# Experts' scatters and gathers interleaved, gate products and a batch's values moved in the slot plan

## The chip, the core and the metric

The kernel runs on one core of a Trainium2 chip. The metric is the device time of one execution in microseconds (us); lower is better. The engines are called as in the profile: PE (TensorE matmul, with its weight load PEld), DVE (VectorE), ACT (ScalarE), POOL (GpSimd) and SP (SyncE, which here issues most of the DMAs).

## What is computed

The input x has 4 batches of 1024 rows with 128 channels. Cut to what matters, the reference is:

```
xn  = layernorm(x)
x   = x + attention(xn) + ffn(xn)

attention: 16 heads of 8 channels; scores q.k + two relative-position terms (63 buckets,
           clipped at +-31), softmax, values + a relative-position value term, projection
ffn:       scores = softmax(xf @ gate_w.T); the 6 best of 64 experts for each row
           xb[e, pos] = xf[tok]                      # at most 64 rows for each expert
           h  = silu(xb @ w1.T) * (xb @ w3.T)        # 64 experts, inner width 88
           y[tok] += (h @ w2.T) * weight             # scatter-add
           z  = silu(xf @ ws1.T) * (xf @ ws3.T) @ ws2.T     # shared expert, width 176
```

All of it is float32.

## The kernel before

Attention is cut into 16 units: unit u is batch u // 4 with four heads, u % 4. `period(u)` issues one unit's work in 32 slots, numbered k = 0 to 31. In every slot PE computes far scores of unit u (p2, exponentiated on ACT at L616) woven with far scores of unit u + 1 (p1, whose row maxima DVE takes at L570). Around these two, a hand-written plan of slots places everything else: values of the unit (`values`, an even slot each), scores near the diagonal (`near_keys`, step "a", and others), masks, row maxima and loads. Every engine works through its own queue in the order in which the program issues to it. So the place of a call in a slot sets the order on PE, DVE, ACT, POOL and in the DMA queues.

Two PSUM pools are passed round: `ps2` with two pairs of banks (p2, the shared expert's pz, a batch's pv, the near products pkb and others) and `ps1` with three single banks (p1, the experts' pxg, ph and py, the shared expert's pzo and others). A buffer is handed out again once its reader has finished.

POOL's queue, in the units with experts, holds these in turn: the masking of rows at slots 4 and 5 (`residues`, L476, products km and qm, which PE's pkb matmuls of slot 9 take), a multiplication of the finished unit (o, L700) at slot 9, the additions of maxima to near scores (nt, L643) at slots 12 and 31, masks again at slots 18 and 19, and the indirect DMAs of the experts.

The 64 experts are done in 16 batches of four, two batches for each unit from 5 on, by `moe(u, k)`, which advances a generator `experts`. An even batch flips its gathered rows (pxg) at slot 27, computes the gates (ph, tanh on ACT, two products on DVE) at slot 31, and in the next unit's slot 2 the outputs (py, scaled on DVE into yw, L324). An odd batch does so at slots 17, 19 and 25. A batch's step at slot 2 or 25 is followed by `load_experts` for the batch after next: three weight loads on SP, then four gathers on POOL (L297). The four scatter-adds into y_rows (L327, on POOL) are issued at slot 6 for an even batch and at slot 26 for an odd one. As they add to the same array, each waits until the one before has landed. The first two batches' loads and eight gathers are issued in unit 5 at slot 20.

The shared expert (`shared`) takes, at slots 3, 5, 7 and 13, a product pz with its gates (tanh on ACT, two products on DVE into zs, L283 to L285), and then pzo. At the head of a batch (u % 4 == 0) the values of the whole batch are computed: `batch_values`, in slots 1, 3, 5, 7, 9 for the far form and 4, 6, 8, 10 for the near one, behind the experts' step of the slot.

Of the kernel before, what the change touches and what calls it, by code (L numbers as in the profile page):

```python
# [11 lines left out]
AF = mybir.ActivationFunctionType  # L12
# [12 lines left out]
E, TOPK, CAP, FI, SI = 64, 6, 64, 88, 176  # L25
# [15 lines left out]
def attention_moe_kernel(ctx: ExitStack, tc: tile.TileContext, ins: dict, out: bass.AP):  # L41
    nc = tc.nc
    pe, act, dve, pool = nc.tensor, nc.scalar, nc.vector, nc.gpsimd
# [3 lines left out]
    def mm(o, lhsT, rhs, start, stop=True):  # L47
        pe.matmul(o, lhsT, rhs, start=start, stop=stop, skip_group_check=True)  # L48
# [39 lines left out]
    xs_d = nc.dram_tensor("xs_rows", (T + 1, C + E), F32).ap()  # L88
# [80 lines left out]
    gather_i = cp.tile([CAP, E], I32, name="gather_i")  # L169
# [110 lines left out]

    def silu_mul(o, h1, h3):

        act.activation(o, h1, AF.Tanh, scale=0.5)  # L283
        dve.scalar_tensor_tensor(o, o, 1.0, h1, ALU.add, ALU.mult)
        dve.scalar_tensor_tensor(o, o, 0.5, h3, ALU.mult, ALU.mult)  # L285

    def load_experts(mp, q):
        es = slice(4 * q, 4 * q + 4)
        w1 = mp.tile([C, 4, FI], F32, tag="w1", name=f"w1_{q}")
        w3 = mp.tile([C, 4, FI], F32, tag="w3", name=f"w3_{q}")  # L290
        w2 = mp.tile([FI, 4, C], F32, tag="w2", name=f"w2_{q}")
        nc.sync.dma_start(w1, ins["w1"][:, es, :])
        nc.sync.dma_start(w3, ins["w3"][:, es, :])
        nc.sync.dma_start(w2, ins["w2"][:, es, :])
        xg = mp.tile([CAP, 4, C + E], F32, tag="xg", name=f"xg{q}")
        for e in range(4):
            pool.indirect_dma_start(  # L297
                out=xg[:, e, :], out_offset=None, in_=xs_d[:, :],
                in_offset=bass.IndirectOffsetOnAxis(ap=gather_i[:, 4 * q + e : 4 * q + e + 1], axis=0),
            )  # L300
        return w1, w3, w2, xg

    def experts(mp, q, w1, w3, w2, xg):

        px = bank(f"pxg{q}")
        for e in range(4):
            flip(px[:, CAP * e : CAP * e + CAP], xg[:, e, 0:C], e == 0)
        xgT = mp.tile([C, 4 * CAP], F32, tag="xgT", name=f"xgT{q}", bufs=1)
        dve.tensor_copy(xgT, px[:, 0 : 4 * CAP])
        yield  # L310
        ph = bank(f"ph{q}").rearrange("p (k x) -> p k x", k=2)
        for k, w in ((0, w1), (1, w3)):
            for e in range(4):
                mm(ph[0:FI, k, CAP * e : CAP * e + CAP], w[:, e, :], xgT[:, CAP * e : CAP * e + CAP], e == 0 and k == 0)
        hs = mp.tile([FI, 4 * CAP], F32, tag="hs", name=f"hs{q}", bufs=1)
        silu_mul(hs, ph[0:FI, 0, :], ph[0:FI, 1, :])
        yield
        py = bank(f"py{q}")
        yw = mp.tile([CAP, 4, C], F32, tag="yw", name=f"yw{q}", bufs=1)
        for e in range(4):  # L320
            mm(py[0:CAP, C * e : C * e + C], hs[:, CAP * e : CAP * e + CAP], w2[:, e, :], e == 0)
        x = C + 4 * q
        for e in range(4):
            dve.tensor_scalar_mul(yw[:, e, :], py[0:CAP, C * e : C * e + C], xg[:, e, x + e : x + e + 1])  # L324
        yield
        for e in range(4):
            pool.indirect_dma_start(  # L327
                out=y_d[:, :], out_offset=bass.IndirectOffsetOnAxis(ap=scatter_i[:, 4 * q + e : 4 * q + e + 1], axis=0),
                in_=yw[:, e, :], in_offset=None, compute_op=ALU.add,
            )  # L330
        yield

    def shared(k):
        b, c = divmod(k, 2)
        xc = xnT[:, b, PAD + 512 * c : PAD + 512 * c + 512]
        for f in range(2):
            zs = wk.tile([FI, 512], F32, tag="zs", name=f"zs{k}_{f}", bufs=1)
            pz = psum(f"pz{k}_{f}")
            for j, w in enumerate((later["ws1"], later["ws3"])):
                mm(pz[0:FI, j, :], w[:, FI * f : FI * f + FI], xc, True)  # L340
            silu_mul(zs, pz[0:FI, 0, :], pz[0:FI, 1, :])
            yield
            po = bank(f"pzo{k}_{f}")
            for t in range(4):
                mm(po[:, C * t : C * t + C], zs[:, C * t : C * t + C], later["ws2"][:, f, :], t == 0)
            xv = xacc[:, 8 * b + 4 * c : 8 * b + 4 * c + 4, :].rearrange("p n c -> p (n c)")
            dve.tensor_tensor(xv, xv, po, ALU.add)
            yield
# [39 lines left out]
    def batch_values(b, ws):  # L388

        flat = lambda t: t.rearrange("p h r -> p (h r)")  # L390
        ones = one9.unsqueeze(1).to_broadcast([P, 4, 36])
        pv = psum(f"pv{b}_{ws[0]}")
        place = lambda i: (pv[:, i // 3, 144 * (i % 3) : 144 * (i % 3) + 144])
        for i, (far, t) in enumerate(ws):
            k0 = PAD + 128 * t if far else 64 * t
            mm(place(i), xnT[:, b, k0 : k0 + 128], later["w_v"], i % 3 == 0)
        for i, (far, t) in enumerate(ws):
            if far:
                dve.tensor_tensor(vf[:, :, t].rearrange("p a h r -> p a (h r)"), place(i).unsqueeze(1).to_broadcast([P, 2, 144]),  # L399
                                  rv_ul.rearrange("p a g r -> p a (g r)"), ALU.add)  # L400
            else:
                dve.tensor_tensor(flat(vn[:, t]).rearrange("p (g r) -> p g r", r=36), place(i).rearrange("p (g r) -> p g r", r=36),
                                  ones, ALU.add)

    def first_values(u):
        for a in range(2):
            dve.tensor_copy(v0s[u % 2][:, a, :, 0:9], vf[:, a, 0, 4 * (u % 4) : 4 * (u % 4) + 4, :])
# [309 lines left out]
    pools = []  # L717
    loaded = {}
# [35 lines left out]
    quads = {}  # L754

    def moe(u, k):

        n = u - 5
        if not 0 <= n <= E // 8:
            return  # L760
        q = {2: -2, 6: -2, 17: -1, 19: -1, 25: -1, 26: -1, 27: 0, 31: 0}.get(k, -E) + 2 * n
        if 0 <= q < E // 4:
            if k in (17, 27):
                quads[q] = experts(pools[0], q, *loaded.pop(q))
            next(quads[q], None)
            if k in (2, 25) and q + 2 < E // 4:
                loaded[q + 2] = load_experts(pools[0], q + 2)
        if k in (3, 5, 7, 13) and n < E // 8:
            if k == 3:
                quads["shared"] = shared(n)  # L770
            next(quads["shared"])
# [43 lines left out]
    def period(u):  # L815
# [10 lines left out]
        for k in range(SLOTS):  # L826
# [16 lines left out]
                last.append(finish_last(u, U, 0))  # L843
            if k in sides:
                next(other, None)
            if k in take_at.get(u, ()):
                next(taking[0], None)
            moe(u, k)
# [11 lines left out]
            if U and k % 2 == 0 and k > 0:  # L860
                values(u, k // 2 - 1)
                if k in (14, 22):
                    tables, products = near_values(u, U, k // 22, wts[u])
                    for emit in tables:
                        emit()
                if k in (16, 24):
                    for emit in products:
                        emit()
            for emit in x:
                emit()  # L870
            r()
# [14 lines left out]
            if U:  # L886
                if k == 1:
                    max_ready(u, U, 1)
                    if V:
                        query_rows(u + 1, V, 1)  # L890
                        replicas(u + 1, V, 0)
                if u % 4 == 0:
                    if k in far_at:
                        batch_values(u // 4, [(True, t) for t in far_at[k]])
                    if k in near_at:
                        batch_values(u // 4, [(False, t) for t in near_at[k]])
                    if k == 1:
                        first_values(u)
                if k == 2:
                    wts[u] = value_table(u)  # L900
                    max_sent(u, U, 1, max_rows(u, U, 1))
                if k == 12:
                    near_shift(u, U, 1)
                    if u == 0:
                        add_bias(0)
                if k in (4, 6, 18, 20):
                    near_exp(u, U, k // 18, k in (6, 20))
# [8 lines left out]
            if u == 5 and k == 20:  # L916
                route_ctx.close()
                pools.append(ctx.enter_context(tc.tile_pool(name="moe", bufs=2)))
                loaded.update({q: load_experts(pools[0], q) for q in range(2)})
            if k == 12 and u + 2 < UNITS:  # L920
                tabs[u + 2] = score_tables(u + 2)
            if k == 30 and u + 2 < UNITS:
# [102 lines left out]
```

## Time and profile before

| | |
|---|---|
| median of 3 runs | 1734.68 us (1733.72 to 1736.65) |
| profiled execution | 1794.26 us |
| its span, first to last instruction | 1792.5 us |
| mean granted TensorE clock in it | 0.961 |
| PE busy | 1654.7 us, 92% of the span |
| DVE, ACT, POOL busy | 57%, 42%, 34% |
| scatters (L327) on POOL | 64, 91.1 us busy, 1424 ns each |
| gathers (L297) on POOL | 64, 59.1 us busy, 923 ns each |
| km (L476) on POOL | 32, 80.2 us busy, 2508 ns each |

The profiled execution is 59.6 us longer than the median of the timed runs. Rows of groups give line, engine, operation, output and input, count, then the busy time and the mean of one in ns, and behind the second bar the idle time of the engine just ahead of them with what ended most of it.

### The profile page before, as it was taken

The page shows a single profiled execution, that of the slowest core. Times are in us where ns is not written, and L with a number is a line of the kernel's source. Part 1 is how long each engine was busy: PE and PEld are TensorE (multiplying, and loading weights), DVE is VectorE, ACT ScalarE, POOL GpSimd, SP SyncE. Part 2 cuts the span into 40 slices and gives each one's busy share as a digit, 9 for nine tenths or more (in the row PEclk, how much of TensorE's full clock was granted, in tenths as well). Part 3 has the DMA queues.
Part 4 walks back from the last instruction along what each step waited for, and adds up shares of the span by engine and source line. Part 5 has one row for each costly group of instructions (what it writes and reads, how often), then busy time and mean ns, then how long its engine had stood idle before and what let it go on. Part 6 is the DMA issues. An engine that isn't in the chain of part 4 may idle for free. (4 is left out here: it accounts for less than half of the span.)

```text
span 1792.5 us, 61397 instructions
## 1 busy us (share of the span) xinstructions
PE 1654.7 (92%) x28106; PEld 1005.9 (56%) x28106; DVE 1030.6 (57%) x1836; ACT 754.3 (42%) x846; POOL 603.0 (34%) x336
## 2 busy tenths in 40 slices
PE   7879989899999997999998999999999899997996
PEld 3645555465656554566565665656656566564652
DVE  5666555666666575554656556555555654554522
ACT  0144434544443452444434345444444433454463
POOL 1042141321457553142333423335252332422330
PEclk8899989999999997999999999999999999998998
DMA  5231331322222132231323223232232322313221
GB/s 143 66 91 44 91 102 42 98 69 69 62 72 72 39 98 60 80 91 50 103 79 84 62 53 103 77 87 74 81 86 64 96 56 71 80 46 102 86 79 31
DMA packets 89002, 136.20 MB, mean 76 GB/s; under 512 B 19156, under 2 KB 57965, under 8 KB 88745
## 3 DMA queue, kind: packets, MB, share of 16 engines
q1 hardware_dynamic: 80137, 126.35, 24.6%
q0 software_dynamic: 7168, 5.25, 2.4%
q8 instruction: 220, 3.60, 0.8%
q10 hardware_dynamic: 1440, 0.70, 0.2%
q14 instruction: 37, 0.30, 0.1%
HBM read 117.68 MB, written 14.55 MB: 74 GB/s over the span
## 5 line engine op out<-in xcount | busy, mean ns | idle before, releaser
L570 DVE TENSOR_REDUCE mx<-p 128x1 f32<-128x480 f32 x992 | 604.2, 650 | 487.7 <-PE p L48 436.5
L616 ACT ACTIVATE et<-p 128x1024 f32<-128x1024 f32 x496 | 507.8, 1025 | 699.4 <-PE p L48 661.3
L48 PE MATMUL p<-qu,kf 32*128 32x512 f32 (+4 forms) x1536 | 332.4, 514 | 37.4 <-DMA qu<-m_rows 7.4
L48 PE MATMUL p<-kf,ql 32*128 32x480 f32 (+8 forms) x1536 | 348.0, 502 | 18.9 <-DVE mx L570 14.8
L48 PE MATMUL p<-ql,kf 32*128 32x512 f32 (+4 forms) x1536 | 312.0, 490 | 13.0 <-DVE xacc L706 5.9
L48 PE MATMUL p<-kf,qu 32*128 32x480 f32 (+8 forms) x1536 | 320.8, 481 | 1.5 <-DVE mx L570 1.5
L643 POOL TENSOR_TENSOR nt<-nt,mb 128x1024 f32<-128x1024 f32 x64 | 154.5, 2425 | 356.6 <-DMA mb<-m_rows 271.5
L48 PE MATMUL acc<-et,vf 128*9 128x512 f32 (+4 forms) x2688 | 245.9, 464 | 2.9 <-DVE vf L399 2.2
L48 PEld LDWEIGHTS p<-qu,kf 32*128 32x128 f32 x1536 | 120.4, 188 | 159.4 <-ACT et L616 40.4
L48 PEld LDWEIGHTS p<-ql,kf 32*128 32x128 f32 x1536 | 132.0, 191 | 80.4 <-issue 27.9
L48 PEld LDWEIGHTS p<-kf,qu 32*128 32x128 f32 x1536 | 142.8, 192 | 23.8 <-issue 11.4
L48 PEld LDWEIGHTS p<-kf,ql 32*128 32x128 f32 x1536 | 133.0, 189 | 39.6 <-DVE mx L570 31.7
L476 POOL TENSOR_TENSOR km<-kr,mask_k 128x1088 f32<-128x1088 f32 x32 | 80.2, 2508 | 190.5 <-DMA kr<-k_rows 177.1
L327 POOL DMA_INDIRECT y_rows<-yw,scatter_i x64 | 91.1, 1424 | 154.8 <-DMA y_rows<-yw,scatter_i 118.1
L502 ACT COPY kb<-pkb 128x1024 f32<-128x1024 f32 x64 | 64.8, 1012 | 162.7 <-PE pkb L48 158.3
L48 PE MATMUL pn<-qm,t 64*128 64x64 f32 x2048 | 130.0, 278 | 0.0
L48 PEld LDWEIGHTS acc<-et,vf 128*9 128x9 f32 x2688 | 51.4, 90 | 139.5 <-issue 127.9
L48 PEld LDWEIGHTS pn<-qm,t 64*128 64x128 f32 x2048 | 121.1, 190 | 10.9 <-issue 10.9
L297 POOL DMA_INDIRECT xg<-xs_rows,gather_i x64 | 59.1, 923 | 198.6 <-issue 145.5
L476 POOL TENSOR_TENSOR qm<-qm,mask_q 128x1024 f32<-128x1024 f32 x32 | 75.5, 2359 | 74.4 <-DMA qm<-q_rows 44.3
L48 PE MATMUL pkb<-kr,qm 64*64 64x64 f32 x4096 | 83.3, 223 | 15.3 <-issue 12.2
L48 PEld LDWEIGHTS pkb<-km,t 64*64 64x64 f32 x4096 | 67.8, 136 | 44.8 <-issue 35.1
(242 smaller groups left out, 1910.3 us busy)
## 6 DMA issues: line engine op xcount, KB each, us to landing
mb<-m_rows SPq DMA_DIRECT2D x64, 512.0 KB
kr<-k_rows SPq DMA_DIRECT2D x64, 272.0 KB
qm<-q_rows SPq DMA_DIRECT2D x64, 256.0 KB
wt<-in_rv_ext SPq DMA_DIRECT2D x16, 1024.0 KB
w<-in_w SPq DMA_DIRECT2D x48, 176.0 KB
rb<-r_rows SPq DMA_DIRECT2D x15, 512.0 KB
t<-in_rk_ext SPq DMA_DIRECT2D x64, 46.0 KB
t<-in_rq_ext SPq DMA_DIRECT2D x64, 46.0 KB
```

The costliest lines, as they stand in the source:

```text
L48: pe.matmul(o, lhsT, rhs, start=start, stop=stop, skip_group_check=True)
L297: pool.indirect_dma_start(out=xg[:, e, :], out_offset=None, in_=xs_d[:, :], in_offset=bass.IndirectOffsetOnAxis(ap=gather_i[:, 4 * q + e : ...
L327: pool.indirect_dma_start(out=y_d[:, :], out_offset=bass.IndirectOffsetOnAxis(ap=scatter_i[:, 4 * q + e : 4 * q + e + 1], axis=0), in_=yw[ ...
L476: pool.tensor_tensor(by8(o), by8(t), mask.unsqueeze(1).to_broadcast([P, t.shape[1] // 8, 8]), ALU.mult)
L502: act.copy(U.kb[p][:, :, :, 64 * gh : 64 * gh + 64], pkb.rearrange("p e (n w) -> p e n w", w=64))
L570: dve.reduce_max(U.mx[:, half, h, n : n + 1], p1[e][:, 0:w], axis=AX.X)
L616: act.activation(et, wide, AF.Exp)
L643: pool.tensor_tensor(U.nt[p, c], U.nt[p, c], mb, ALU.add)
```

## The change

Three things move. First, a batch's step at slot 2 or 25 now issues the loads of the batch after next, and then its four scatters, each followed by one gather for the batch after next; slots 6 and 26 no longer hold scatters. Second, the tanh of the gates is separated from the two DVE products, which are issued one slot later: for the experts at slots 20 and 0 (in place of 19 and 31), for the shared expert at slots 4 and 8 (in place of 3 and 7). Third, `batch_values` and `first_values` stand ahead of the experts' step in their slot. The gathers of the first two batches are issued by the same new function.

```diff
     def silu_mul(o, h1, h3):
 
-        act.activation(o, h1, AF.Tanh, scale=0.5)
         dve.scalar_tensor_tensor(o, o, 1.0, h1, ALU.add, ALU.mult)
         dve.scalar_tensor_tensor(o, o, 0.5, h3, ALU.mult, ALU.mult)
...
         xg = mp.tile([CAP, 4, C + E], F32, tag="xg", name=f"xg{q}")
-        for e in range(4):
-            pool.indirect_dma_start(
-                out=xg[:, e, :], out_offset=None, in_=xs_d[:, :],
-                in_offset=bass.IndirectOffsetOnAxis(ap=gather_i[:, 4 * q + e : 4 * q + e + 1], axis=0),
-            )
         return w1, w3, w2, xg
+
+    def gather(q, e, xg):
+        pool.indirect_dma_start(
+            out=xg[:, e, :], out_offset=None, in_=xs_d[:, :],
+            in_offset=bass.IndirectOffsetOnAxis(ap=gather_i[:, 4 * q + e : 4 * q + e + 1], axis=0),
+        )
...
         hs = mp.tile([FI, 4 * CAP], F32, tag="hs", name=f"hs{q}", bufs=1)
+        act.activation(hs, ph[0:FI, 0, :], AF.Tanh, scale=0.5)
+        yield
         silu_mul(hs, ph[0:FI, 0, :], ph[0:FI, 1, :])
         yield
...
-        yield
+        if q + 2 < E // 4:
+            loaded[q + 2] = load_experts(mp, q + 2)
         for e in range(4):
             pool.indirect_dma_start(
                 out=y_d[:, :], out_offset=bass.IndirectOffsetOnAxis(ap=scatter_i[:, 4 * q + e : 4 * q + e + 1], axis=0),
                 in_=yw[:, e, :], in_offset=None, compute_op=ALU.add,
             )
+            if q + 2 < E // 4:
+                gather(q + 2, e, loaded[q + 2][3])
         yield
...
+            act.activation(zs, pz[0:FI, 0, :], AF.Tanh, scale=0.5)
+            yield
             silu_mul(zs, pz[0:FI, 0, :], pz[0:FI, 1, :])
             yield
...
-        q = {2: -2, 6: -2, 17: -1, 19: -1, 25: -1, 26: -1, 27: 0, 31: 0}.get(k, -E) + 2 * n
+        q = {0: -2, 2: -2, 17: -1, 19: -1, 20: -1, 25: -1, 27: 0, 31: 0}.get(k, -E) + 2 * n
         if 0 <= q < E // 4:
             if k in (17, 27):
                 quads[q] = experts(pools[0], q, *loaded.pop(q))
-            next(quads[q], None)
-            if k in (2, 25) and q + 2 < E // 4:
-                loaded[q + 2] = load_experts(pools[0], q + 2)
-        if k in (3, 5, 7, 13) and n < E // 8:
+            next(quads[q])
+        if k in (3, 4, 5, 7, 8, 13) and n < E // 8:
...
+            if U and u % 4 == 0:
+                if k in far_at:
+                    batch_values(u // 4, [(True, t) for t in far_at[k]])
+                if k == 1:
+                    first_values(u)
             if k in take_at.get(u, ()):
                 next(taking[0], None)
             moe(u, k)
...
+            if U and u % 4 == 0 and k in near_at:
+                batch_values(u // 4, [(False, t) for t in near_at[k]])
             for emit in x:
                 emit()
             r()
...
-                if u % 4 == 0:
-                    if k in far_at:
-                        batch_values(u // 4, [(True, t) for t in far_at[k]])
-                    if k in near_at:
-                        batch_values(u // 4, [(False, t) for t in near_at[k]])
-                    if k == 1:
-                        first_values(u)
...
-                loaded.update({q: load_experts(pools[0], q) for q in range(2)})
+                for q in range(2):
+                    loaded[q] = load_experts(pools[0], q)
+                    for e in range(4):
+                        gather(q, e, loaded[q][3])
```

## Prediction

> **What bounds the kernel now.** I read the page from the top: engines, clock, groups, then the waits, the tiles that the change moves, and last the timelines of POOL and PE in one unit.
>
> ```profile
> span 1792.5 us, 61397 instructions
> PE 1654.7 (92%) x28106; PEld 1005.9 (56%) x28106; DVE 1030.6 (57%) x1836; ACT 754.3 (42%) x846; POOL 603.0 (34%) x336
> L327 POOL DMA_INDIRECT y_rows<-yw,scatter_i x64 | 91.1, 1424 | 154.8 <-DMA y_rows<-yw,scatter_i 118.1
> L476 POOL TENSOR_TENSOR km<-kr,mask_k 128x1088 f32<-128x1088 f32 x32 | 80.2, 2508 | 190.5 <-DMA kr<-k_rows 177.1
> L297 POOL DMA_INDIRECT xg<-xs_rows,gather_i x64 | 59.1, 923 | 198.6 <-issue 145.5
> ```
>
> PE sets the time (92%); POOL is two thirds idle. The 118.1 us in which scatters wait for the landing of the scatter before them are POOL's idle time, so removing them is worth nothing by itself. Two things can count: what else stands in POOL's queue, and what PE waits for. The rows of the mask product km say who waits for it now ("us, times"):
>
> ```profile
> who waited for it (us, times):
>   PEld pkb L48: 3.8, 3
>   PE pkb L48: 3.1, 2
> ```
>
> So PE nearly never waits for km and its partner qm. How near it is, the POOL timeline of unit 9 shows (start, duration, idle before):
>
> ```profile
> 1092.71 0.95 POOL L297 DMA_INDIRECT xg<-xs_rows,gather_i  x1 [3.19 <-DVE yw L324]
> ...
> 1096.42 0.91 POOL L297 DMA_INDIRECT xg<-xs_rows,gather_i  x1 [0.30 <-issue]
> 1103.01 2.48 POOL L476 TENSOR_TENSOR km<-kr,mask_k 128x1088 f32<-128x1088 f32 x1 [5.68 <-DMA kr<-k_rows]
> 1105.45 2.36 POOL L476 TENSOR_TENSOR qm<-qm,mask_q 128x1024 f32<-128x1024 f32 x1
> 1107.97 1.46 POOL L327 DMA_INDIRECT y_rows<-yw,scatter_i  x1 [0.17 <-issue]
> 1116.27 1.45 POOL L327 DMA_INDIRECT y_rows<-yw,scatter_i  x1 [6.84 <-DMA y_rows<-yw,scatter_i]
> 1119.54 1.40 POOL L327 DMA_INDIRECT y_rows<-yw,scatter_i  x1 [1.82 <-DMA y_rows<-yw,scatter_i]
> ```
>
> Today: four gathers, km, qm, and only then the scatters. PE's timeline has the product of kr and qm at 1110.62, 2.8 us after qm ends. The same distance is 1.9, 3.6, 9.9, 2.8, 2.1, 3.2, 11.4 and 0.1 us in units 6 to 13. The third thing to see is PE beside the gathers, in unit 5 (eight of them in a row) and unit 9:
>
> ```profile
> 709.53 0.48 PE L48 MATMUL pkb<-kr,qm 64*64 64x64 f32 x3 [0.97 <-issue]
> 713.08 0.48 PE L48 MATMUL pkb<-kr,qm 64*64 64x64 f32 x4 [1.14 <-issue]
> 705.80:719.50 13.70, 9.38 (x155) 5.51 (x158) 1.22 (x2) 2.04 (x2) 4.59 (x6) 0.50 0.19 52
> ```
>
> Matmuls drip out three or four at a time, with nothing on record to wait for, and then the clock (the fourth number from the right of the last group, 0.50) stands at half. Measured from the first score matmul of one slot to that of the next, unit 5's slot 21 takes 14.33 us against 3.27 in other units (11 lost). Slot 27 takes 6.12 us on average in units 6 to 12, where four gathers come just ahead, against 2.26 in unit 13, which has scatters there but no gathers; slot 28 takes 3.42 against 2.04. That is 5.2 us in seven units, 37 us. The even batch's four gathers, in slots 2 to 4, cost PE under 1 us.
>
> **The change part by part.**
>
> **POOL's order at slot 2, a loss.** Four scatters (1.42 us each to issue) and, alternating with them, four gathers (0.91) now stand ahead of km and qm in POOL's queue, because they are issued at slot 2 and the masks at slots 4 and 5. SP's order is unchanged: the three weight loads stay at slot 2. Each scatter waits for the one before. Uncontended, scatters follow each other every 3.25 us (the odd batch, 1170.74 to 1173.99), and a gather fits between. So the chain ends 0.3 + 3 x 3.25 + 1.4 + 0.3 + 0.9 = 12.7 us after yw is done; in unit 13, without gathers, 11.5. Then km and qm, 2.48 + 2.36 us. To be in time for the product the chain may take 13.5, 13.3, 19.9, 13.3, 13.0, 13.2, 19.9 and 9.1 us in units 6 to 13 (product's start, less yw's end, less 4.9). So uncontended it fits everywhere but in unit 13 (2.4 us lost). But in 1092.7 to 1100 the loads of kr, qm and the weights take a DMA share of 0.58, and under 0.45 the first scatter above landed 6.84 us after its issue ended where 1.8 is usual: 5 us more, a chain of 17.7. Between 12.7 and 17.7 I take 16.7, near the contended row since the share is higher still. Loss: 16.7 - 13.3 = 3.4 us in units 6, 7, 9, 10 and 11 (17 us), none in 8 and 12, 15.5 - 9.1 = 6.4 in unit 13: +23 us. Bounds: 2.4 us (uncontended), and 45 (two landings late by 5 us, and half clock after each stall). Behind km and qm wait PE (pkb), then ACT's copy kb and the next tiles; o and nt on POOL come at slots 9 and 12 and move with them.
>
> **POOL's order at slots 20 and 25.** Odd batches: the scatters start and end about 5 us earlier, since no four gathers (4.9 us) stand ahead of them, and nobody waits, nt follows at slot 31. The gathers stand 3.25 us apart instead of 1.24. If PE's stall grows with their density, most of 37 us goes; if it is a price for each gather (37/28 = 1.3 us), nothing. The rule that speaks against a gain is the Trainium skill's, page SBUF — State Buffer, section Who interferes with whom: "DMA never contends with a compute engine." By it, gathers cannot be what stalls PE, and spreading them is worth 0. The rows above (14.33 against 3.27, only beside gathers) speak against the rule as far as the profiled execution goes. But that execution is 59.6 us longer than the median, and the stalls found (37 + 11) are most of that: they may be there only while the profiler records. The trace can't tell. Between 0 and -30 I take -10: half for that doubt, and part for the price per gather. The half clock that follows (page TensorE: Matmul & The Clock Gate, Part 1: half clock after about 3.4 us of idleness) is in the 37 already; this trace's 0.50 lasts 3.4 or 6.8 us after each stall of unit 6 to 12, though PE idles there for far less than 3.4 us in one piece. By the rule alone only a wait for km of 3.4 us or more would cost a further 1.7 us (half of one such stretch; five units, 8.5); by the row, a shorter one might too. I leave it to the range.
>
> **The first eight gathers** (unit 5) stay in one row, ahead of nothing that is late: 0.
>
> **The products of the gates one slot later.** For the shared expert, PE's waits for zs are small now:
>
> ```profile
> PEld p L48 <- DVE zs L285: 11.2, 15, 1.8
> DVE zs L284 <- ACT zs L283: 18.0, 14, 1.4
> ```
>
> The tanh (0.59 us on ACT) now has a slot to itself, so DVE doesn't stand for it (18.0 us in all, off the path). The PSUM pair pz is released later by about a slot, and the products (0.68 us each) land just ahead of pzo, which may wait 0.5 us, twice a unit: -1 and +1, so 0, bounds -3 and +5. For the experts, products move to slots 20 and 0, which are short on PE (2.03 and 2.17 us) while DVE has a maximum (1.3 us for two of 650 ns) and two products of about 0.4 us there: PE waits for the released bank about 0.4 us, 2 x 8 times: +6 (0 to 12).
>
> **A batch's values ahead of the experts' step.** Only units 0, 4, 8, 12. In units 8 and 12 slots 3 and 7 take 5.13 and 5.25 us against 2.94 and 3.00 elsewhere, slot 9 about 5.2 against 3.62. The values' PSUM pair and DVE copies no longer stand behind zs: about 1 us less in slots 3 and 7, 0.5 in slot 9, 0.6 more in slots 4 and 8, and 1 less in unit 0. -4 (-8 to +2).
>
> Sum: +23 - 10 + 0 + 6 - 4 = +15 us. On the profiled execution, 1794.26 + 15 = 1809; on the median, 1734.68 + 15, so 1750.
>
> **The rivals.**
> - *Km late (likeliest, 0.66).* As summed. Own range 1738 to 1774. For it: slack of 2 to 4 us in five units, and a 6.84 us landing under less load. Against it: kr arrives at 1103 anyway, so the first 10 us of the chain are free.
> - *Faster (0.23): the spread gathers free PE.* Slots 27 and 28 fall to about 3 and 2 us, in timed runs too: 7 x 4.3 = 30 us gained; the chain stays under 13.3 us, so 2.4 lost; 6 - 4 for the rest. 1734.7 - 30 + 2.4 + 2 = 1709; half the relief gives 1724. It decides where the chain after yw stays under 13.3 us. For it: 14.33 against 3.27. Against: even gathers, as dense, cost nothing.
> - *Nothing much (0.11): the waits were POOL's own.* The chain takes 13 to 14 us, PE stalls of 1 us, and they cancel with a little relief: 2.4 + 5 + 6 - 4 - 10 = -1, so 1734, within 1729 and 1741.
> - *The change doesn't do what it says:* a gather may not fit between two scatters, since its own descriptors queue behind. Then scatters come every 4 us and the chain is 14.9: 1.6 us late in five units, 8 + 2.4 + 6 - 4 - 10 = +2, so 1737; its chance is in the third case.
>
> **How the numbers follow.** A difference of 0.2% (3.5 us) is about what a measurement of this kernel can tell from none. Likeliest 1750. The range takes in the half-relief end of the faster case and the stalls with half clock: 1715 to 1774, with about 1 in 10 left out on each side. Faster: 0.23 and a little of the third case, 0.25; same: 0.08; slower: 0.67.
>
> **What would show it.** In the profile after: the rows of km or qm should name pkb as waiting some 20 us in all (now 7); POOL's timeline in units 6, 7, 9, 10, 11 should show the last gather 15 us or more after yw; slot 9 on PE should be 6 to 7 us in these instead of 3.6. Slot 27 at 6 us still means no relief, at 2.5 full relief. Slots 20 and 0 should be 0.4 us longer. I am wrong if km still waits for kr's landing in those units, or if the timed runs gain although the profile shows km late.

## The result and the profile after

The changed kernel takes 1775.43 us (1770.70 to 1781.27) against 1734.46 us for the kernel before: ratio 1.0237, 95% interval 1.0206 to 1.0269, that is 41 us slower. The forecast was 15 us slower, 1750. The direction was right, the size was not.

One fact is needed to read every number below: the kernel before takes 1734 to 1736 us on three of the five chips used for the experiments and 1782 us on the other two, so each kernel is compared only with the kernel before on the same chip, and "on the 1734 us chips" or "on the 1782 us chips" says which. The execution profiled ahead of the prediction (1794.26 us) looks like the second kind: its slots 27 and 28 are long, as theirs are.

From the page of the changed kernel, its span, its busy times and two groups (line, engine, operation, count, then busy us, mean ns, then the idle time ahead and what ended most of it):

```profile
span 1779.5 us, 61417 instructions
PE 1638.8 (92%) x28106; PEld 999.9 (56%) x28106; DVE 1032.3 (58%) x1836; ACT 755.4 (42%) x846; POOL 603.5 (34%) x336
L330 POOL DMA_INDIRECT y_rows<-yw,scatter_i x64 | 91.2, 1426 | 267.0 <-DVE yw L326 186.6
L48 PE MATMUL pkb<-km,t 64*64 64x64 f32 x4096 | 80.8, 231 | 33.0 <-POOL km L483 28.0
```

The last row is new on the page. The rows of km say who waited for it (us, times):

```profile
who waited for it (us, times):
  PEld pkb L48: 30.4, 8
  PE pkb L48: 28.0, 8
```

Before, these rows had 3.8 and 3.1. (PEld and PE wait for the same events, so the two are not added.) POOL's timeline in unit 9, the place that the prediction worked on (start, duration, engine, what, idle before it):

```profile
1075.12 1.43 POOL L330 DMA_INDIRECT y_rows<-yw,scatter_i  x1 [2.25 <-DVE yw L326]
1076.85 0.93 POOL L298 DMA_INDIRECT xg<-xs_rows,gather_i  x1 [0.30 <-issue]
1080.93 1.43 POOL L330 DMA_INDIRECT y_rows<-yw,scatter_i  x1 [3.15 <-DMA y_rows<-yw,scatter_i]
1082.66 0.93 POOL L298 DMA_INDIRECT xg<-xs_rows,gather_i  x1 [0.30 <-issue]
1086.33 1.43 POOL L330 DMA_INDIRECT y_rows<-yw,scatter_i  x1 [2.74 <-DMA y_rows<-yw,scatter_i]
...
1091.23 0.93 POOL L298 DMA_INDIRECT xg<-xs_rows,gather_i  x1 [0.30 <-issue]
1092.16 2.49 POOL L483 TENSOR_TENSOR km<-kr,mask_k 128x1088 f32<-128x1088 f32 x1
1094.60 2.37 POOL L483 TENSOR_TENSOR qm<-qm,mask_q 128x1024 f32<-128x1024 f32 x1
```

km no longer waits for a landing: it starts in the moment in which the last gather has been issued, 16.6 us after yw (1075.6). PE stands there:

```profile
1094.71 1.16 PE L48 MATMUL pkb<-km,t 64*64 64x64 f32 x64 [2.96 <-POOL km L483]
1097.02 2.09 PE L48 MATMUL pkb<-kr,qm 64*64 64x64 f32 x64 [1.15 <-POOL qm L483]
1092.00:1098.00 6.00, 2.14 (x97) 2.01 (x101) 1.23 (x3) 0.89 (x1) 4.95 (x3) 0.83 0.49 152
```

PE waits 2.96 us for km and 1.15 for qm. The same 64 products that took 1.14 us before take 2.09: the granted clock is at 0.50 from 1096.0 to 1102.8, right behind the wait (third row: the stretch, busy us of PE, PEld, DVE, ACT and POOL, then the granted clock, 0.83 in the mean).

The kernel before was profiled again, now on a 1734 us chip (label e2_before). Its POOL and PE timelines beside the odd batch's gathers of unit 9:

```profile
span 1734.0 us, 61397 instructions
1127.30 0.95 POOL L297 DMA_INDIRECT xg<-xs_rows,gather_i  x1 [22.00 <-issue]
...
1131.00 0.90 POOL L297 DMA_INDIRECT xg<-xs_rows,gather_i  x1 [0.31 <-issue]
1130.29 0.43 PE L48 MATMUL p<-qu,kf 32*128 32x192 f32 x2
1131.35 0.46 PE L52 MATMUL pxg<-ident,xg 64*128 64x64 f32 x4
1132.76 0.54 PE L48 MATMUL p<-qu,kf 32*128 32x320 f32 x2
```

The gathers are issued as closely as ever, and slot 27 takes 2.47 us (1130.29 to 1132.76), not the 6.12 of the profile that the prediction read. The stall that the odd chain was to relieve isn't there on these chips. In the same unit, yw is done at 1055.7, km waits for kr, and both products follow on PE without a wait:

```profile
1065.56 2.49 POOL L476 TENSOR_TENSOR km<-kr,mask_k 128x1088 f32<-128x1088 f32 x1 [4.96 <-DMA kr<-k_rows]
1068.00 2.37 POOL L476 TENSOR_TENSOR qm<-qm,mask_q 128x1024 f32<-128x1024 f32 x1
1072.08 1.16 PE L48 MATMUL pkb<-km,t 64*64 64x64 f32 x64
1073.06 1.14 PE L48 MATMUL pkb<-kr,qm 64*64 64x64 f32 x64
```

Two profiles of one kind of chip can be compared slot by slot. Slot times are read off PE's timeline (from a slot's first score matmul to the next slot's). The table gives the differences from e2_before, summed over units 6 to 13, in us:

```
                        slot 9  slot 10  1+4+5+8+21  slots 3+7  slot 15   all slots
changed kernel            32.8      6.0         7.0       -3.5     -4.2        38.8
changed, again (e2)       33.8      5.0         7.0       -3.8     -4.2        38.0
```

Of 41 us, slots 9 and 10 (km and qm late, then half clock) hold 39.

### The profile page after: what moved, and what is told of

Its sections match the earlier page's. It is cut to its first block, busy times and chain, and to the rows that moved or that the text cites. A ratio compares the mean times of both kernels' runs of the same rounds, so it can differ in the third digit from the quotient of the medians.

```text
span 1779.5 us, 61417 instructions
## 1 busy us (share of the span) xinstructions
PE 1638.8 (92%) x28106; PEld 999.9 (56%) x28106; DVE 1032.3 (58%) x1836; ACT 755.4 (42%) x846; POOL 603.5 (34%) x336
## 5 line engine op out<-in xcount | busy, mean ns | idle before, releaser
L48 PE MATMUL p<-kf,ql 32*128 32x480 f32 (+8 forms) x1536 | 336.0, 494 | 8.0 <-DVE mx L577 6.5
L48 PE MATMUL p<-ql,kf 32*128 32x512 f32 (+4 forms) x1536 | 306.9, 485 | 13.2 <-DVE xacc L713 6.2
L48 PE MATMUL p<-kf,qu 32*128 32x480 f32 (+8 forms) x1536 | 316.7, 482 | 1.9 <-DVE mx L577 1.5
L650 POOL TENSOR_TENSOR nt<-nt,mb 128x1024 f32<-128x1024 f32 x64 | 150.5, 2363 | 340.8 <-DMA mb<-m_rows 293.2
L48 PE MATMUL acc<-et,vf 128*9 128x512 f32 (+4 forms) x2688 | 242.1, 461 | 2.9 <-DVE vf L406 2.2
L48 PEld LDWEIGHTS p<-kf,ql 32*128 32x128 f32 x1536 | 128.8, 187 | 24.3 <-DVE mx L577 20.2
L48 PEld LDWEIGHTS pkb<-km,t 64*64 64x64 f32 x4096 | 71.7, 143 | 73.7 <-issue 38.4
L48 PE MATMUL pkb<-km,t 64*64 64x64 f32 x4096 | 80.8, 231 | 33.0 <-POOL km L483 28.0
```

The lines of the kernel that those rows point to most:

```text
L650: pool.tensor_tensor(U.nt[p, c], U.nt[p, c], mb, ALU.add)
```

## Experiments

Theory Q: km and qm stand behind the even batch's chain of scatters and gathers in POOL's queue. Rivals: theory S, that the late gate products cost; theory G, that PE's stall beside gathers in a row decides part of the comparison; within Q, theories L (landings) and P (POOL's own issue work), and W and K on what the landings wait for.

### One part of the change at a time, on a 1782 us chip

e1_pool_only has the chains alone: gates' products and values go back to where they were (the lines below show the products; the values' calls and the slot numbers move back likewise).

```diff
         act.activation(hs, ph[0:FI, 0, :], AF.Tanh, scale=0.5)
-        yield
         silu_mul(hs, ph[0:FI, 0, :], ph[0:FI, 1, :])
...
             act.activation(zs, pz[0:FI, 0, :], AF.Tanh, scale=0.5)
-            yield
             silu_mul(zs, pz[0:FI, 0, :], pz[0:FI, 1, :])
```

> Only the scatter-gather chains at slots 2 and 25 are changed; the gates' products and the batch's values are issued as before. Theory Q (km and qm late behind the even chain: in the profile after, PE's slot 9 is 4.5 to 6.0 us longer in units 6, 7, 9, 10, 11, 13, 31.7 in sum, and slot 10 a further 6 at half clock): 35 to 38 us over before, about 1770. Theory S (the late products are what costs): under 5 us over before. Rival R (the chains help and the rest hurts): below before.

Measured: 1784.28 us beside 1781.82, ratio 1.0011 (0.9995 to 1.0026). Not 1770. But its slot table says why: against e2_before slot 9 is longer by 35.0 us and slot 10 by 5.6, the loss of Q; and slots 27 and 28 are without the 35 us by which they are longer in the first profile of before. Loss and gain cancel on this chip. By its time alone, theory S or "no effect" would have passed.

e1_no_pool is the complement, products and values moved, gathers and scatters as before.

```diff
+        apart = True
         if q + 2 < E // 4:
             loaded[q + 2] = load_experts(mp, q + 2)
+        if apart:
+            if q + 2 < E // 4:
+                for e in range(4):
+                    gather(q + 2, e, loaded[q + 2][3])
+            yield
```

> The change without the chains: gathers at slots 2 and 25, scatters at 6 and 26 as before; products one slot later and a batch's values first. Theory Q: within -3 and +6 us of before, from the slot table of after: slots 1, 4, 8, 21 longer by 0.34, 0.17, 0.12, 0.26 in eight units (+7), a batch's units shorter by about 1.5 in slots 3 to 9, twice (-3). Theory S: +30 or more.

Measured: 1811.45 us, ratio 1.0138 (1.0095 to 1.0181): a miss, some 30 us over before where -3 to +6 was expected, and for theory S if one stops here. Against e2_before the excess lies in slots 4 (15.1 us), 5 and 6 (11.6), and in 27 and 28 (27.0, already in before on such chips): beside the even gathers at slots 2 to 4, which in before had cost next to nothing. Whether it belongs to the moved products or to the chip is taken up below (e4_silu_only).

e1_odd_only puts only the odd batch's chain into the kernel before (products and values as in e1_pool_only, and in the diff just shown):

```diff
-        apart = True
+        apart = q % 2 == 0
```

> Before, with the chain only at slot 25 (odd batches); even batches, products and values as before. If the stall of PE beside four gathers in a row (slot 27: 6.1 us against 2.3) belongs to every execution: 30 us faster than before, about 1705. If it is there only in some executions, such as the profiled one of before: within 3 us of before, while its profile is 30 us shorter than that of before. Theory Q expects no loss here, since nobody waits for the odd chain.

Measured: 1753.03 us, ratio 0.9825 (0.9787 to 0.9863): 29 us faster. So the stall is no artifact of profiling: timed runs of these chips have it, and it goes when each gather stands behind a scatter that waits (slot 27 takes 2.5 to 2.7 us in units 6 to 12). On the 1782 us chips the term that the prediction took at -10 is -29.

e1_even_late is the change whole, but the even chain waits until slot 6, behind km and qm.

```diff
             loaded[q + 2] = load_experts(mp, q + 2)
+        if q % 2 == 0:
+            yield
```

> The change whole, but the even batch's chain at slot 6, behind km and qm, with the weight loads still at slot 2. Theory Q: the 38 us are gone, within -3 and +8 us of before; slot 9 at 3.7 us in units 6 to 11. The gathers of the even batch land by slot 12 and are read at slot 27, so no new wait. Theory S or a price of interleaving itself: still 30 us or more over before.

Measured: 1780.84 us, ratio 0.9979 (0.9959 to 1.0000). Slot 9 is nearly back (8.3 over), but slots 11 to 13 are 20.3 us longer: the chain's gathers now run there, beside other near products. A second place where this chip is slow beside gathers, and here they are spread, each behind a scatter, while the even gathers of before, four in a row, cost PE under 1 us: so closeness alone doesn't decide, and what does isn't shown. On the other kind of chip see e4_even_late.

### The whole again, and what makes the chain long, on a 1734 us chip

e2_after and e2_before are the two kernels unchanged.

> The changed kernel itself again. Theory Q+G (km and qm late behind the even chain cost 38 us; PE's stall beside four gathers in a row, which the odd chain removes, is worth 30 us where before has it, nothing where before runs without it): about 1775 to 1782 us either way; beside a before of 1782 the ratio is 1.00, beside a before of 1734 it is 1.024. A theory in which the change itself costs 41 us wherever it runs expects 1.024 beside either.

> The kernel before, for its profile in these executions. If it takes 1775 to 1795 us, slot 27 shows 5.5 to 6.5 us in units 6 to 12 as in the first profile; if it takes 1734 us, theory G expects 2.5 there, and slot 21 of unit 5 at 3 to 5 us instead of 14.

Measured: 1775.65 us beside 1734.52, ratio 1.0246 (1.0226 to 1.0267); e2_before 1734.57 us, and its profile, shown above, has slot 27 at 2.5 us in units 6 to 12 and slot 21 of unit 5 at 3.4. Theory G's half of this holds: where before runs at 1734, there is no stall to relieve.

e2_four_y sends the four scatters of a batch to four arrays, so that none waits for another; it leaves out setting the three new arrays to zero and adding them to the output.

```diff
+    y_4 = [y_d] + [nc.dram_tensor(f"y_rows{e}", (T + CAP, C), F32).ap() for e in range(1, 4)]
...
-                out=y_d[:, :], out_offset=bass.IndirectOffsetOnAxis(...),
+                out=y_4[e][:, :], out_offset=bass.IndirectOffsetOnAxis(...),
```

> The changed kernel with the four scatters of a batch going to four arrays, so that none waits for the landing of the one before; left out: only the first array is added to the output. POOL's order is unchanged. Theory L (the landings make the chain long): chain of 4 x (1.42 + 0.91 + 0.6) = 11.7 us after yw instead of 16.5, km in time in units 6, 7, 9, 10, 11, so 25 to 35 us below the changed kernel. Theory P (POOL's own issue work ahead of km suffices): less than 8 us below.

Measured: 1729.25 us, ratio to before 0.9965 (0.9951 to 0.9979), 46 us below the changed kernel, more than expected. POOL in unit 9:

```profile
1058.03 1.42 POOL L331 DMA_INDIRECT y_rows<-yw,scatter_i  x1 [2.07 <-DVE yw L327]
...
1066.92 1.42 POOL L331 DMA_INDIRECT y_rows<-yw,scatter_i  x1 [0.30 <-issue]
1068.65 0.93 POOL L299 DMA_INDIRECT xg<-xs_rows,gather_i  x1 [0.30 <-issue]
1069.59 2.49 POOL L484 TENSOR_TENSOR km<-kr,mask_k 128x1088 f32<-128x1088 f32 x1
```

The same eight DMAs in the same order ahead of km take 11.1 us after yw (1058.5) instead of 16.6, and slot 9 is back in every unit (-0.1 us in sum against before). It is the landings, theory L. POOL's issue work alone fits. The 5 us below before come from unit 13, whose last slot is 5.9 us shorter: the load of y there follows only a quarter of the scatters. That is a gain of the four arrays and not of the change.

e2_weights_late moves the three weight loads of even batches from slot 2 to slot 10.

```diff
+        if q < 2 or q % 2:
+            weights()
+        later_w[q] = weights
...
         yield
+        if q % 2 == 0 and q + 2 < E // 4:
+            later_w[q + 2]()
+        yield
```

> The changed kernel with the even batch's three weight loads at slot 10 instead of slot 2. Theory W (the landing that takes 6 to 9 us in the even chain waits behind the weight loads): chain of 12.7 us, slot 9 back to 4 us, 25 to 35 us below the changed kernel. Theory K (it waits behind the loads of kr and qm, which stand ahead anyway): chain 15 to 16.5 us, under 8 us below.

Measured: 1775.46 us, ratio to before 1.0254 (1.0228 to 1.0279): as slow as the changed kernel. Its POOL timeline in unit 10 still has the long landing:

```profile
1185.01 0.93 POOL L304 DMA_INDIRECT xg<-xs_rows,gather_i  x1 [0.30 <-issue]
1191.92 1.43 POOL L336 DMA_INDIRECT y_rows<-yw,scatter_i  x1 [5.98 <-DMA y_rows<-yw,scatter_i]
```

Theory W is out: the 0.5 MB of weights don't make the chain long (with them moved it takes 15.3 to 17.4 us in units 6, 7, 9, 10 and 11).

### What the landings wait for, and the small parts, on a 1782 us chip

e3_small_kr cuts the loads of kr and qm ahead of the even chain to an eighth.

```diff
+            m = 128 if p == 0 and 7 <= u <= 14 else n
+            if m < n:
+                dve.memset(t[:, m:n], 0.0)
             for e in range(2):
-                nc.sync.dma_start(t[64 * e : 64 * e + 64, :],
+                nc.sync.dma_start(t[64 * e : 64 * e + 64, 0:m],
```

> The changed kernel with the loads of kr and qm at slot 1 of units 6 to 13 cut from 1064 or 1024 columns to 128, the rest of the two tiles filled by DVE (1 us each); left out: all but 128 columns of km and qm there. Theory K (the slow landing in the even chain waits behind these loads): chain of 12.7 us after yw, slot 9 back at 4 us, 25 to 35 us below the changed kernel. Rival (a scatter lands slowly whatever else is loaded, or behind the weights): chain still 15 us or more, under 8 us below.

Measured: 1773.55 us beside 1782.25 (0.9971, 0.9953 to 0.9989). The expected distance to the changed kernel can't be read from this, since that was timed on the other chips. The chain can. In unit 10:

```profile
1184.92 1.43 POOL L330 DMA_INDIRECT y_rows<-yw,scatter_i  x1 [0.79 <-DMA y_rows<-yw,scatter_i]
1186.66 0.93 POOL L298 DMA_INDIRECT xg<-xs_rows,gather_i  x1 [0.30 <-issue]
1188.10 1.43 POOL L330 DMA_INDIRECT y_rows<-yw,scatter_i  x1 [0.52 <-DMA y_rows<-yw,scatter_i]
```

Scatters follow each other every 3.1 to 3.4 us here, km starts 11.5 to 13.0 us after yw in units 6 to 12, and slot 9 takes 3.65 to 3.68 us in units 6, 7, 10 and 11 (8.2 to 9.3 in the changed kernel), 4.9 in unit 9. It isn't the kind of chip: e1_pool_only, with the whole loads on a 1782 us chip, has km 16.5 to 18.3 us after yw in units 6, 7, 9, 10 and 11. That is theory K: the slow landings ahead of km come with the loads of kr and qm. One unit doesn't fit: in unit 13 the chain took 18.7 us, its last scatters 5.5 and 8.8 us apart, and slot 9 15.8. What was loaded there isn't settled.

e3_silu_only has the late gate products alone, e3_bv_only a batch's values alone; each is the changed kernel with the other parts undone as in the diffs above.

> Before with only the gates' products one slot later. From the slot tables of the two whole kernels in matching executions: slots 1, 4, 8 and 21 longer by 2.3, 1.8, 1.9 and 2.1 us over all units, slot 5 shorter by 1.1: +7 us where PE has no stall beside gathers. Where it has one, the shift can bring the even gathers onto PE's work, as in the kernel without the chains (slots 4 to 6 up to 4.5 us longer in five units): +20 to +30.

> Before with only a batch's values in front. As predicted: -4 us (0.9 in slot 3 and 1.0 in slot 7 of units 8 and 12, the rest in slot 9 and unit 0). A theory in which its PSUM pair now delays the experts' step: +2 or more.

Measured: products 1803.70 us beside 1782.25, ratio 1.0107 (1.0076 to 1.0139), within the second of its two expectations; values 1783.25, ratio 1.0007 (0.9993 to 1.0021), no change. In the first, PE in unit 6 waits in slot 4 beside the even gathers (759.5 to 764.2):

```profile
763.11 1.05 PE L48 MATMUL acc<-et,vf 128*9 128x192 f32 x16
766.64 0.54 PE L48 MATMUL p<-qu,kf 32*128 32x320 f32 x2 [2.47 <-ACT et L629]
```

e3_best was meant as the version to keep: the odd chain, a batch's values in front, and the first eight gathers of unit 5 one in a slot.

```diff
-                for q in range(2):
-                    loaded[q] = load_experts(pools[0], q)
-                    for e in range(4):
-                        gather(q, e, loaded[q][3])
+                loaded.update({q: load_experts(pools[0], q) for q in range(2)})
+                firsts.extend((q, e, loaded[q][3]) for q in range(2) for e in range(4))
+            if firsts:
+                gather(*firsts.pop(0))
```

> The parts that cost nothing on POOL's way to km: the odd batches' chain at slot 25 and a batch's values in front as in the changed kernel; even batches (gathers at slot 2, scatters at 6) and the gates' products as before; and the first eight gathers one in a slot, from slot 20 of unit 5. Theory Q+G: 3 to 5 us faster than before where before takes 1734, 40 us faster where before takes 1782 (30 of the odd chain, 10 of the first gathers), about 1730 to 1745 in either.

Measured: 1754.11 us, ratio 0.9835 (0.9809 to 0.9861): 28 us, not 40. The first gathers were not spread at all:

```profile
704.11 1.11 POOL L298 DMA_INDIRECT xg<-xs_rows,gather_i  x1 [10.94 <-PE p L48]
705.51 0.94 POOL L298 DMA_INDIRECT xg<-xs_rows,gather_i  x1 [0.30 <-issue]
...
712.81 0.90 POOL L298 DMA_INDIRECT xg<-xs_rows,gather_i  x1 [0.30 <-issue]
```

Eight in a row as ever, and slot 21 of unit 5 at 14.25 us. A slot is a place in the program; POOL has nothing else in its queue there and runs ahead. The odd chain spreads its gathers only because each stands behind a scatter that has to wait.

### The same parts on a 1734 us chip

> The changed kernel again. Theory Q+G: 1772 to 1782 us whatever before takes; beside a before of 1734 that is 1.024, beside a before of 1782 it is 1.00 (38 us lost at slot 9 and 10, 37 us won at slots 27 and 28). A theory in which the chip is simply slower by 2.7% where before takes 1782 expects 1820 there.

Measured: 1778.37 us beside 1736.35, ratio 1.0232 (1.0207 to 1.0257). The whole change itself was never timed on a 1782 us chip. What it would take there isn't shown: the chains alone are even (e1_pool_only), the products alone cost 21 us (e3_silu_only).

> Before with only the gates' products one slot later, as once before beside a before of 1782, where it cost 21 us. Beside a before of 1734: +7 us, from slots 1, 4, 8 and 21. If the cost of 21 us is its own and not that of PE's stall beside the gathers: +20 there too.

Measured: 1743.42 us, ratio 1.0038 (1.0025 to 1.0051), that is 6.6 us. The products cost 7 us by themselves; the rest of the 21 goes with the kind of chip, and in e3_silu_only it lies mostly in slot 4, beside the gathers, and in slot 6. DVE's timeline in unit 10 shows the two products hs between the maxima of slot 20 and those of slot 21, and PEld where PE waits in slot 21:

```profile
1221.44 1.21 DVE L583 TENSOR_REDUCE mx<-p 128x1 f32<-128x480 f32 x2
1222.58 0.41 DVE L283 SCALAR_TENSOR_TENSOR hs<-hs,ph 88x256 f32<-88x256 f32 x1
1223.02 0.42 DVE L284 SCALAR_TENSOR_TENSOR hs<-hs,ph 88x256 f32<-88x256 f32 x1
1223.45 1.22 DVE L583 TENSOR_REDUCE mx<-p 128x1 f32<-128x480 f32 x2
1222.71 0.29 PEld L48 LDWEIGHTS p<-kf,ql 32*128 32x128 f32 x2 [0.17 <-DVE mx L583]
```

PE waits for the second maximum of slot 20 (done at 1222.65), which stands ahead of hs. Why it now needs that bank, a candidate being that ph holds one of the three single banks a slot longer, the runs don't show.

> Before with the odd chain at slot 25 and a batch's values in front; nothing else of the change. Theory Q+G: beside a before of 1734, -3 us (the values), about 1731; beside a before of 1782, -30 us, about 1752.

Measured: 1741.09 us, ratio 1.0010 (0.9994 to 1.0026): no gain where there is no stall, and the 3 us of the values are not to be seen.

> The changed kernel with the even chain at slot 6, behind km and qm. Beside a before of 1782 it stood at 1781, with slots 9 to 12 longer by up to 4 us next to its gathers. Theory Q+G: beside a before of 1734 these are not longer, and the time is 1734 to 1740, that is 36 to 41 us below the changed kernel. If the chain costs PE time wherever it stands: 1755 or more.

Measured: 1745.85 us, ratio 1.0043 (1.0027 to 1.0058), 33 us below the changed kernel. Its slot 9 is 1.0 us over before and its slots 11 to 13 0.7; what is left is the products' 7 us. On these chips the even chain costs PE time only where km stands behind it.

### A version that keeps the chain, and the values once more, on a 1734 us chip

e5_two_y lets the scatters go by turns to two arrays, both added at the end.

```diff
-                out=y_d[:, :], out_offset=bass.IndirectOffsetOnAxis(...),
+                out=y_2[e % 2][:, :], out_offset=bass.IndirectOffsetOnAxis(...),
...
+        for n, d in enumerate(y_2):
+            y = wk.tile([P, 8, C], F32, tag="mb", name=f"y{b}_{n}", bufs=MB)
+            nc.sync.dma_start(y, rows_of(d, b))
+            pool.tensor_tensor(xv, xv, y, ALU.add)
```

> Before with the chains of the change at slots 2 and 25 and a batch's values in front, the gates' products as before, and the scatters going by turns to two arrays that are both added to the output at the end (one load of 512 KB and one POOL addition of 2.4 us more for each of the four batches). A scatter waits only for the last but one, so theory L expects the even chain at 12 to 14 us, km just in time, and against the changed kernel 35 to 45 us less: 1725 to 1738 beside a before of 1734 (the chain without its loss, -6 of the early scatters at the last expert unit, +3 for the additions). Beside a before of 1782: 1750. Rival: two landings in turn are as slow as one, chain 16 us, 1765 or more.

Measured: 1750.85 us, ratio 1.0083 (1.0055 to 1.0111). km starts 11 to 14 us after yw in units 6 to 12, slot 9 is 6.1 us over before instead of 33, and unit 13 wins 8 us as hoped; but the second array's zeroing makes unit 1 longer by 8 us, and what lies behind unit 13, with the second additions, by some 7 (its span is 14.6 us over that of e2_before, of which units 0 to 13 hold 7.1). The landing half of the expectation held, the sum did not.

> Before with only a batch's values in front, as once before beside a before of 1782 (ratio 1.0007). Predicted -4. From the slots of the last traces beside a before of 1734: -2.4 us in units 8 and 12, +1.6 in unit 0 (slots 5 and 6 give back what slots 1 to 3 win): -1, so no change that can be told.

Measured: 1737.73 us, ratio 1.0009 (0.9996 to 1.0022): no change.

No kernel run here, with the computation complete, beats the kernel before on both kinds of chip. The odd chain alone (e1_odd_only) is worth 1.75% where before takes 1782 us, and with the values (e4_odd_bv) it can't be told from before where that takes 1734.

## Why the prediction was right or wrong

The direction and the main mechanism, km late behind the even chain, were right. Three steps failed: the relief of the odd gathers, put at -10, was 0; the time that the even chain may take, put at 13.3 us, is 12.4; and the half clock that comes with each wait for km was left out of the sum. Slots 9 and 10 together lost 39 us where +23 was forecast.

- **POOL's order at slot 2.** Right in mechanism and place, too small in size: +23 against 33 to 34 at slot 9, and 5 to 6 more at slot 10. The chain's length, forecast as 16.7 us, was 16.5 to 17.9 in units 6, 7, 9, 10 and 11. The term that failed is the 13.3 us that it "may take": worked out from the profile at hand, in which PE was slower between yw and pkb. In e2_before the product starts 17.3 to 17.4 us after yw in those units, so the chain may take 12.4 (12.4 to 12.5). That is almost 1 us for each of five units. Slot 9 then loses 4.5 to 6.9, not 3.4, part of it since the products behind the wait already run at half clock. The half clock was left to the range. In the changed kernel's trace the granted clock falls to 0.50, during the wait for km or at most 1.3 us after it, in all six units with a stall (6, 7, 9, 10, 11 and 13) and in neither of 8 and 12. It stays there for 3.4 to 10.2 us; where that outlasts slot 9, slot 10 is longer too, by 0.6 to 1.8 us in four of the six. By the rule of the Trainium skill's page TensorE: Matmul & The Clock Gate, Part 1 (about 3.4 us of idleness), as the prediction read it, units 7 and 9 would have been spared: their longest single waits are 2.95 and 2.96 us. By the row that the prediction set beside it a shorter wait may cost it too, and that is what the trace shows.
- **The odd gathers.** This term failed: -10 was taken, it was 0. The prediction noted that the 48 us of stalls were most of the distance between the profiled execution and the median, and still gave the relief half a weight. The doubt was justified, its reason was wrong: not the profiler makes the stall, for timed runs have it or not with the chip (e1_odd_only, timed, -29; e4_odd_bv, +2 and not told from 0). The Trainium skill's rule that DMA never contends with a compute engine (page SBUF — State Buffer, section Who interferes with whom) agrees with the 1734 us chips, where slot 27 takes 2.48 us beside four gathers. On the others the 29 us speak against it, though no run tells the gathers' transfers from their issue on POOL.
- **The gates' products.** +6 forecast, +6.6 measured (e4_silu_only), and the match is luck. The experts' products, forecast at +6 in slots 20 and 0, cost 4.5 in slots 1 and 21 (2.4 and 2.2 us); the shared expert's, forecast at 0, cost 2.6 in slots 4 and 8 (1.8 and 1.9), less 1.1 in slot 5.
- **A batch's values.** -4 forecast, 0 measured. Slots 3 and 7 of units 8 and 12 fell by 0.3 to 1.0 us each as said (-3.2 in e5_bv_only), slot 9 by nothing, and unit 0, where 1 us was to be won, lost 2.6: slots 4 to 6 give back 3.6 us, more than the 2.4 that slots 1 to 3 win.
- **Not seen:** slot 15 of unit 13, 4.2 us shorter than in e2_before, since its scatters are done earlier: in e2_before PE waits there for o (2.31 us), which stands on POOL behind the last even scatter. The gain varies: kernels with these scatters at slot 6 have the slot at 7.2 to 11.2 us on the 1734 us chips, the changed kernel at 6.7.
- **The sum** with sizes as measured is 34 + 5 + 0 + 7 - 4 - 4 = 38, and 2 of unit 0: 40 of 41.
- **The rivals.** "Faster" named the right point, the chain under 13.3 us: e2_four_y meets it with 11.1 and wins the whole loss back. That a gather may not fit between two scatters was wrong: between undisturbed landings it fits (3.1 to 3.4 us).

## What to carry to other kernels

Before work is moved ahead in an in-order queue, list what stands behind the new place and how late its readers let it be; a chain of DMAs that wait on each other's landings is priced by the transfers that are under way at that point, not by its issue time. Check that a profile and the timed median belong to the same behaviour before a stall in the profile is counted as something to be won: here 60 us between the two were the warning, and slack read from the slow one was too large as well. Putting instructions into different slots of the program doesn't spread them in time unless something in their queue makes them wait.

## What the hardware showed

The same program takes 1734 us on some chips and 1782 on others. Each chip was used on one occasion, so that the chip makes the difference, and not the occasion, isn't shown. The traces put most of it beside gathers: of the 58.5 us between the two profiles of before, 35 lie in slots 27 and 28 and 11 in slot 21 of unit 5. In the first profile of before, DVE in unit 9 starts a maximum at 1170.13 whose input PE had finished by 1167.9, and PE stands still for its bank (the row's own columns as above):

```profile
1170.13 1.22 DVE L570 TENSOR_REDUCE mx<-p 128x1 f32<-128x480 f32 x2 [5.08 <-remote]
1170.84 0.53 PE L48 MATMUL p<-kf,ql 32*128 32x320 f32 x1 [1.20 <-DVE mx L570]
```

On a 1734 us chip, the same maximum starts at once:

```profile
1129.46 1.22 DVE L570 TENSOR_REDUCE mx<-p 128x1 f32<-128x480 f32 x2 [2.95 <-PE p L48]
```

So in this place DVE starts about 2 us after its input is done on record, and the profile names no engine of this core that held it ("remote" ends 36.9 us of such waits in the first profile of before, none in e2_before). A completion that reaches DVE late would look like this. It doesn't cover everything: in the stall of unit 5, PE stops with nothing on record to wait for. What causes either, and why on some chips only, is not settled by these runs.

A scatter of 64 rows landed in 2.8 to 3.0 us from its issue as a rule. It took 8.4 us while about 1 MB of loads for kr and qm was under way (the second scatter of unit 10 in e2_weights_late), and 9.2 us beside the loads of rb and mb (the fourth scatter of unit 10 in the changed kernel).
